# Layer 0's middle taps from a copy moved by GpSimd, and the attention's entrance in another order

## The chip, the cores and the metric

One core of one Trainium2 chip runs the whole program. The metric is the time of one execution on the device in microseconds, lower is better. The kernel before took 947.2 us, the median of three runs (946.99 to 947.26).

## What is computed

The input is x, 16 images of 256 channels and 28 x 28 pixels in fp32. Four layers follow each other:

- Layer 0: a 3x3 convolution of sign(x) with the signs of the weights, scaled by each output channel's mean absolute weight, then a batch norm over all images and pixels, plus x.
- Layer 1: signs, a 3x3 convolution, a 1x1 convolution, PReLUs and two gates made from channel means.
- Layer 2: two convolutions of signs like layer 0's, each with PReLU and a batch norm around it, plus the layer's input, and a last PReLU.
- Layer 3: attention over the 784 pixels of an image with 64 channels for queries, keys and values, and a projection back to 256 channels, plus its input.

```python
def _L3_conv_ref(x, Wq, Wk, Wv, Wp):
    xf = x.reshape(B, C, N)
    q = jnp.einsum('rc,bcn->bnr', Wq, xf)
    k = jnp.einsum('rc,bcn->brn', Wk, xf)
    v = jnp.einsum('rc,bcn->bnr', Wv, xf)
    attn = jax.nn.softmax(jnp.einsum('bnr,brm->bnm', q, k) * scale, axis=-1)
    out = jnp.einsum('bnm,bmr->brn', attn, v)
    return jnp.einsum('cr,brn->bcn', Wp, out).reshape(B, C, H, W) + x
```

A batch norm over all images means that a layer's last moments must be known before the next layer's first image can be made. The stretches between layers are therefore serial.

## The kernel before

**Tiles.** Channels lie on the 128 partitions, in two halves (k = 0, 1). A pixel half is 14 rows, 392 columns (`HN`); an image has two. B = 16, S = 28.

**Convolutions of signs** (`sign_layer`, line 384, used by layer 0 and twice by layer 2). The signs of image i lie as fp16 in `fpads[:, i % 2]`, 30 x 30 with a border of zeros. An image takes 36 matmuls of 392 columns: two channel halves, three rows of taps, three taps c in a row, two pixel halves (line 404). Tap c reads the padded rows from column c on, so the middle tap (c = 1) begins at an odd fp16 column. Two output channels are packed in one sum (`PACK`), which `apart` (line 411) takes apart: ScalarE evicts from PSUM (L420), VectorE makes the other half (L422). `conv_ps` has three PSUM buffers. With `shifted`, images from `direct` on read the middle tap from a second tile that holds the same signs moved by one column, so that it begins at an even one; SyncE makes this copy with a DMA (L434), and the middle taps are then multiplied last within an image (line 398). Layer 2 passes `shifted` in both convolutions, from image 4 and from image 2 on. Layer 0 does not.

**Order.** In `sign_layer` the order on TensorE, ScalarE, VectorE and SyncE is that of the program (`manual_schedule`): for each block the products, the next image's signs, the batch statistics of the block before (`post`), the preparation of later weights (`steps`), and `apart`. GpSimd is not in that set: a scheduler orders its queue. In layer 0, `post0` (line 682) computes batch statistics on VectorE and stores the eviction with a DMA from GpSimd's queue (L688, `n0d`).

**Between layers.** `keep_busy(n)` (line 502, and line 1475 in the attention) multiplies n tiles of zeros on TensorE. Layer 1's tail has several (lines 1108 to 1190), among them `keep_busy(14)` at line 1179 ahead of the matmul of `hidden_a`. `norm` (line 238) makes scale and shift of layer 2's last batch norm: `bn_aggr`, a variance, `rsqrt` (line 144: a Sqrt on ScalarE, a reciprocal and one Newton step on VectorE), then the shifts on ScalarE (L264).

**The attention's entrance** (`attend_unshifted`, from line 1636; here all five engines keep the program's order). Image 0 is finished in two pixel halves: scale, shift, the layer's input x2 and PReLU (lines 1640 to 1649), then queries and keys in one product per half (`queries_keys`, L1486). `keep_busy(8)` follows, then the copies of queries (L1493) and keys (L1497) out of PSUM, `scores(0, 0)` (L1509, with the exponentials at L1513), the values (`project_v`, L1580; four groups of output columns side by side) and their transpose (`turn_v`). Keys lie in chunks of 112 pixels, seven per image. In the loop over images, `scores` of seven chunks, `values` (L1530), sums of exponentials (`sum_up`: chunks 0 to 3 on GpSimd, 4 to 6 on VectorE), denominators and projection are interleaved with the next image's queries, keys and values. `finish_a` (line 1461) scales an image on ScalarE and, from image 2 on, has a DMA from GpSimd's queue add x2 to it (L1466); `finish_b` (line 1468) applies the PReLU on VectorE. The PSUM tag `sc` has two buffers.

Of the kernel before, what the change touches and what calls it, by code (L numbers as in the profile page):

```python
# [27 lines left out]
F32 = mybir.dt.float32  # L28
# [11 lines left out]
P = 128  # L40
B = 16
# [25 lines left out]

STEEP = 1e24


# [20 lines left out]
def forward(ctx: ExitStack, tc: tile.TileContext, d: dict, out: bass.AP, careful: bool):  # L91
# [37 lines left out]

    doubts = const.tile([P, 4 * NB + 10], F32, name="doubts")  # L130
    nc.gpsimd.memset(doubts, 0.0)
# [11 lines left out]

    def rsqrt(name, v, half=None, beside=None):

        r, t = (const.tile(list(v.shape), F32, name=name + q) for q in ("_r", "_t"))
        A.activation(t, v, AF.Sqrt)
        if beside:
            beside()
        V.reciprocal(r, t)  # L150
        tt(t, r, r, ALU.mult)
        if half is not None:
            tt(r, r, half, ALU.mult)
        else:
            V.tensor_scalar(r, r, -0.5, None, ALU.mult)
        tt(t, t, v, ALU.mult)
        V.scalar_tensor_tensor(r, t, -3.0, r, ALU.add, ALU.mult)
        return r
# [78 lines left out]

    def norm(name, moments, gamma, beta, sf=None, then=lambda r: None, late=False):


        half, e = vtile(name + "_half"), vtile(name + "_e")
        V.tensor_scalar(half, gamma, -0.5, None, ALU.mult)
        if sf is not None:

            tt(e, sf, sf, ALU.mult)
            V.tensor_scalar(e, e, 1e-30, 1.0 / EPS, ALU.max, ALU.mult)
            V.reciprocal(e, e)
        m, var = moments()
        v, c, less = vtile(name + "_v"), vtile(name + "_c"), vtile(name + "_less") if late else None
        if sf is not None:  # L250
            tt(v, var, e, ALU.add)
        else:
            V.tensor_scalar(v, var, EPS, None, ALU.add)
        r = rsqrt(name, v, half, (lambda: V.tensor_scalar(less, m, -1.0, None, ALU.mult)) if late else None)
        then(r)
        if not late:
            tt(c, m, r, ALU.mult)
            return r, tt(c, beta, c, ALU.subtract)

        def shift(b):  # L260
            o = vtile(f"{name}_shift{len(made)}")
            made.append(o)
            for k in range(2):
                A.activation(o[:, k:k + 1], r[:, k:k + 1], AF.Identity, bias=b[:, k:k + 1], scale=less[:, k:k + 1])  # L264
            return o

        made = []
        return r, shift
# [114 lines left out]

    def sign_layer(pads, w, temp, room, sign, post, steps, moments, blocks, together=1, shifted=None, direct=2):

# [8 lines left out]
        def products(*js):  # L394
            for j in js:
                pss[j] = conv_ps()
            moved = shifted is not None and blocks[js[0]][0] >= direct
            for taps in ((0, 2), (1,)) if moved else ((0, 1, 2),):
# [29 lines left out]
        def sign_image(i):  # L428

            for r0, r1 in ((0, HR + 1), (HR + 1, S)) if i == 0 else ((0, S),):  # L430
                load = sign(i, slice(r0, r1), lambda k: inner(pads[:, i % 2], k, r0, r1))
                if shifted is not None and i >= direct:
                    to, of = (t[:, i % 2].rearrange("p k a b -> p (k a b)") for t in (shifted, pads))
                    nc.sync.dma_start(out=to[:, 0:-1], in_=of[:, 1:])  # L434
                if load:
                    load()
# [57 lines left out]
    with tc.tile_pool(name="ps_conv", bufs=3, space=PSUM) as psc, \  # L494
# [13 lines left out]
        with tc.tile_pool(name="ph1", bufs=1) as ph:  # L508

            fpads = sign_pads(ph, "vs") if careful else sign_pads(const, None)  # L510
            xs, ns = [None] * B, [None] * B

# [178 lines left out]
            mom = block_moments("l0", PARTS)  # L691
            sign_layer(fpads, w0, temp, room0, sign0, post0, steps, mom, whole_images(PARTS), together=2 if careful else 1)
            for b in range(2):
# [424 lines left out]
            with tc.manual_schedule(engines={ET.PE, ET.DVE, ET.Activation, ET.SP}):  # L1118
# [59 lines left out]
                unit_b(b, 1)  # L1178
                keep_busy(14)
                for k in range(2):  # L1180
# [32 lines left out]
        with tc.tile_pool(name="ph2", bufs=1) as ph:  # L1213
# [36 lines left out]

            def post2(order, alpha, mom, doubt):

# [3 lines left out]
                def post(block, ab):  # L1256
# [33 lines left out]

                    squares = [lambda h=h, m=m: square(h, m) for h, _, m in pieces(block) if not careful]
                    squares_p = [lambda s=s: square_p(*s) for s in by_sums]
                    if i < B - 1:
# [22 lines left out]
            if not careful:  # L1316
# [11 lines left out]
                fpads, w2b, temp, room2, lambda i, rows, out: sign2(pt[i], sg2, bg2, rows, out),  # L1328
                post2(range(B), pv("a2"), mom, doubts[:, 3 * NB:4 * NB]), [], mom, PARTS, shifted=shifted,
            )  # L1330
            late_squares()

            if careful:
                keep_busy(45)
                sg3, bg3 = norm("l2c", mom, pv("g3"), pv("b3"), sf2)
                tt(bg3, bg3, cc, ALU.add)
            else:
                keep_busy(35)
                with tc.manual_schedule(engines={ET.DVE, ET.Activation}):
                    sg3, shift3 = norm("l2c", mom, pv("g3"), pv("b3"), sf2, late=True)  # L1340
                    bg3 = shift3(b3c)
# [78 lines left out]
def attend_unshifted(ctx, tc, d, out, wqk, wv, wp, keys, worst, doubts, flag, pv, finish):  # L1420
# [61 lines left out]

    def queries_keys(b, h, ps):

        for k in range(2):
            T.matmul(  # L1486
                ps[:, h, :HN], lhsT=wqk[:, k, :], rhs=x[b][:, k, h * HN:(h + 1) * HN], start=(k == 0), stop=(k == 1)
            )

    def queries(b, h, ps):  # L1490
# [3 lines left out]

    def keys_to(b, rows, h, ps):
        copy = A.copy if rows else V.tensor_copy
        copy(  # L1497
            keys[b % 2][64 * rows:64 * rows + 64, :, 2 * h:2 * h + 2, 0:GC].rearrange("p c g i -> p g c i"),
            ps[64:P, h, :HN].rearrange("p (g c i) -> p g c i", g=2, i=GC),
        )  # L1500
# [13 lines left out]

    def sum_up(b, *cs):

        for c in cs:
            late, e = c > 3, es[b, c]
            if c in (1, 5):
                sums[b, late] = buf(f"sum{c}", 2)  # L1520
                (V if late else nc.gpsimd).tensor_tensor(sums[b, late], es[b, c - 1], e, ALU.add)
            elif c in (2, 3, 6):
                (V if late else nc.gpsimd).tensor_tensor(sums[b, late], sums[b, late], e, ALU.add)  # L1523

# [49 lines left out]

    def project_v(b):
        ps = one_bank(pssm, "sm")
        for a in range(2):
            for k in range(2):
                for g in range(4):
                    T.matmul(  # L1580
                        ps[32 * g:32 * g + 32, a * GN:(a + 1) * GN], lhsT=wv[:, k, 32 * a:32 * a + 32],
                        rhs=x[b][:, k, g * GN:(g + 1) * GN], start=(k == 0), stop=(k == 1),
                    )
        A.copy(
            vt[:, :, :, 0:GC].rearrange("p c a i -> p a c i"),
            ps[:, 0:2 * GN].rearrange("p (a c i) -> p a c i", a=2, i=GC),
        )
# [48 lines left out]
    with tc.manual_schedule(engines={ET.PE, ET.Activation, ET.DVE, ET.Pool, ET.SP}):  # L1636

        ps = [two_banks(psmi, "mi"), two_banks(pssc, "sc")]
        cuts = [slice(h * HN, h * HN + HN) for h in range(2)]
        for n in cuts:  # L1640
            v = x[0][:, 1, n]
            V.scalar_tensor_tensor(v, v, sg3[:, 1:2], x2[0][:, 1, n], ALU.mult, ALU.add)
        for h, n in enumerate(cuts):
            finish_a(0, n, (0,))
            v, w = (x[0][:, k, n] for k in range(2))
            A.activation(w, w, AF.Identity, bias=bg3[:, 1:2])
            V.tensor_tensor(v, v, x2[0][:, 0, n], ALU.add)
            for k, y in enumerate((v, w)):
                V.scalar_tensor_tensor(y, y, alpha[:, k:k + 1], y, ALU.mult, ALU.max)
            queries_keys(0, h, ps[h])  # L1650
        A.activation(ph.tile([P, 2], F32, name="e"), sg3, AF.Exp, scale=0.0)
        keep_busy(8)
        for h in range(2):
            keys_to(0, 1, h, ps[h])
            queries(0, h, ps[h])
            keys_to(0, 0, h, ps[h])
        finish_a(1)
        scores(0, 0)
        project_v(0)
        finish_b(1, ks=(0,))  # L1660
        turn_v(0)
        finish_b(1, ks=(1,))
        V.transpose(ones.rearrange("p a i -> p (a i)"), turned.rearrange("p a i -> p (a i)"))
        for b in range(B - 1):
            scores(b, 1)
            if b > 0:
                take_values(b - 1)
            if b == 0:
                finish_a(2)
            if b > 1:  # L1670
                project(b - 2, 0)()
            sum_up(b, 1)
            scores(b, 2)
            if b > 0:
                sum_up(b - 1, 6)
            scores(b, 3)
            sum_up(b, 2, 3)
            ps = two_banks(psmi, "mi")
# [17 lines left out]
            if b + 3 < B:  # L1696
                finish_a(b + 3)
            for c in range(4):
                values(b, c)
# [260 lines left out]
```

## Time and profile before

| what | value |
|---|---|
| median of three runs | 947.2 us |
| the profiled execution: time | 948.88 us |
| the profiled execution: span, first to last instruction | 947.1 us |
| mean granted clock of TensorE | 0.996 |
| busy TensorE, VectorE, ScalarE, GpSimd | 98%, 80%, 71%, 15% of the span |
| layer 0's convolution | 10.46 to 109.20 us |
| layer 1 with what precedes it | 109.20 to 464.20 us |
| layer 2's two convolutions | 464.20 to 560.70 and 566.25 to 662.40 us |
| attention with its entrance | 662.40 to 947.1 us |

PE is TensorE, PEld its weight loads, ACT ScalarE, DVE VectorE, POOL GpSimd, SP SyncE. A line of the timeline has start and duration in us, engine, source line, operation, what it writes and reads, its shape, how many were merged, and in brackets the idle time before it with what ended that. In a table by stretches, each engine has its busy time and the number of its instructions.

### The profile page before, as it was taken

To read this page: it belongs to the slowest core of one execution; us is meant where nothing else is said; L and a number is where in the kernel's file an instruction comes from. 1 tells how busy PE (TensorE), PEld (TensorE's weight loads), DVE (VectorE), ACT (ScalarE), POOL (GpSimd) and SP (SyncE) were. 2 spreads that over 40 slices of the span, in tenths; PEclk is the share of its full clock that TensorE was granted. 3 is DMA by queue.
4 is the path that set the end of the run, shared out by engine and by line. 5 is a ranking of instruction groups with operands and counts; after the bars stand their busy time and mean duration, and the time that the engine had idled before them with its cause. 6 is when DMAs were issued, how large, how long until landed. Compare 5 with 4: busy or idle time off the path is not lost.

```text
span 947.1 us, 15041 instructions
## 1 busy us (share of the span) xinstructions
PE 930.2 (98%) x5626; PEld 583.6 (62%) x5632; DVE 759.9 (80%) x1446; ACT 676.1 (71%) x1184; POOL 139.0 (15%) x158
## 2 busy tenths in 40 slices
PE   7999999999999999999999999999999999999996
PEld 3555578888788888887555565556444444444442
DVE  3877888999998889987888887889656868777676
ACT  5766578888888788874777767776766666676653
POOL 2001100000000000000000000000235353443422
PEclk9999999999999999999999999999999999999999
DMA  9877533454543344320566201111142433425212
GB/s 334 292 284 272 187 121 122 173 186 177 198 163 139 139 157 163 143 112 35 207 241 214 113 40 60 79 79 59 31 73 70 97 108 81 125 69 136 69 63 112
DMA packets 39733, 130.70 MB, mean 138 GB/s; under 512 B 4882, under 2 KB 16852, under 8 KB 39652
## 3 DMA queue, kind: packets, MB, share of 16 engines
q1 hardware_dynamic: 33332, 98.31, 28.8%
q0 software_dynamic: 5632, 30.54, 11.8%
q8 instruction: 46, 0.75, 0.3%
q10 hardware_dynamic: 688, 0.80, 0.2%
q14 instruction: 35, 0.29, 0.1%
HBM read 72.67 MB, written 32.11 MB: 111 GB/s over the span
## 4 chain that ended last, share of the span: by engine, by line
PE 95%; DVE 2%; ACT 1%; DMA 1%; issue 0%; SPq 0%; DVEq 0%; ACTq 0%
PE cv L404 31%; PE cv L810 29%; PE sc L1509 8%; PE av L1530 8%; PE cv L937 5%; PE mi L1486 5%; PE sm L1580 2%; PE unused L506 2%; PE mi L1598 2%; PE sm L1530 1%; PE gate L905 1%; DMA st<-in_w_dram 1%; PE hid L713 1%; DVE r L1564 1%; DVE p L1609 0%
## 5 line engine op out<-in xcount | busy, mean ns | idle before, releaser
L810 PE MATMUL cv<-vs,w 128*128 128x392 f32 (+1 forms) x1296 | 272.4, 352 | 0.3 <-DVE vs L141 0.3
L404 PE MATMUL cv<-fpads,wpk 128*128 128x392 f16 (+1 forms) x1458 | 249.3, 327 | 2.2 <-DVE wpk L329 1.2
L404 PEld LDWEIGHTS <-wpk 128*128 128x128 f16 x1782 | 172.1, 97 | 123.6 <-issue 4.3
L810 PEld LDWEIGHTS cv<-vs,w 128*128 128x128 f32 x768 | 143.2, 190 | 6.3
L1513 ACT ACTIVATE es<-sc 128x784 f32<-128x784 f32 x112 | 87.4, 823 | 40.0 <-PE sc L1509 40.0
L810 PEld LDWEIGHTS <-w 128*128 128x128 f16 x768 | 69.4, 99 | 51.9 <-issue 9.1
L1509 PE MATMUL sc<-q,keyswa 64*128 64x392 f32 x448 | 89.9, 513 | 1.2 <-ACT es L1513 0.9
L1530 PE MATMUL av<-es,v 128*64 128x392 f32 x448 | 80.7, 499 | 0.0
L1268 DVE SCALAR_TENSOR_TENSOR p<-ab,vec 128x392 f32<-128x392 int16 (+1 forms) x132 | 78.1, 605 | 0.0
L420 ACT ACTIVATE ab<-cv 128x392 int16<-128x392 f32 (+1 forms) x66 | 32.1, 486 | 56.1 <-PE cv L404 53.2
L1523 POOL TENSOR_TENSOR sum<-sum,es 128x784 f32<-128x784 f32 x32 | 67.2, 2101 | 2.5
L1509 PEld LDWEIGHTS sc<-q,keyswa 64*128 64x128 f32 x448 | 38.9, 186 | 44.0 <-issue 17.1
L404 PE MATMUL cv<-shifted,wpk 128*128 128x392 f16 (+1 forms) x324 | 60.6, 322 | 0.0
L810 PE MATMUL cv<-one_on,w 128*128 128x392 bf16 x240 | 59.4, 329 | 0.0
L965 POOL DMA_DIRECT2D x2d<-x x16 | 8.6, 536 | 345.3 <-DVE x L959 285.0
L1497 DVE COPY keyswa<-mi 64x392 f32<-64x392 f32 x31 | 16.3, 564 | 53.2 <-ACT q L1493 53.2
L1530 PEld LDWEIGHTS av<-es,v 128*64 128x64 f32 x448 | 29.4, 136 | 47.0 <-issue 46.6
L422 DVE SCALAR_TENSOR_TENSOR ab<-ab,cv 128x392 int16<-128x392 int16 (+1 forms) x66 | 36.1, 547 | 27.5 <-ACT ab L420 26.6
L792 ACT CAST vs<-vs 128x840 fp32r<-128x840 bf16 x63 | 54.1, 883 | 2.5 <-DVE vs L141 2.3
L937 PE MATMUL cv<-z,fw 128*128 128x392 f32 x256 | 48.9, 342 | 0.1
L937 PEld LDWEIGHTS cv<-z,fw 128*128 128x128 f32 x256 | 46.1, 188 | 0.9 <-ACT z L929 0.9
L1486 PE MATMUL mi<-p,wqk 128*128 128x392 f32 x124 | 45.1, 506 | 0.1
(325 smaller groups left out, 1532.9 us busy)
## 6 DMA issues: line engine op xcount, KB each, us to landing
xs<-in_x_dram SPq DMA_DIRECT2D x30, 784.0 KB, 5.0
one_on<-vs SPq DMA_DIRECT2D x60, 209.8 KB, 2.9
x2d<-x POOLq DMA_DIRECT2D x16, 784.0 KB, 3.6
out_dram<-p SPq DMA_DIRECT2D x15, 784.0 KB, 3.6
shifted<-fpads SPq DMA_DIRECT2D x26, 449.8 KB, 2.8
p<-x2d POOLq DMA_DIRECT2D x14, 784.0 KB, 6.8
p<-x2d SPq DMA_DIRECT2D x13, 784.0 KB, 5.8
n0d<-n POOLq DMA_DIRECT2D x16, 392.0 KB, 4.4
```

The costliest lines, as they stand in the source:

```text
L404: T.matmul(pss[j][:, n // size if careful else h, :rows * S].rearrange("p (a b) -> p a b", b=S), lhsT=w[:, n, c, :], rhs=src[:, blocks[j][ ...
L420: A.activation(by_halves(ab[:, 1], blocks[j]), ps, AF.Copy, scale=1.0 / PACK)
L422: V.scalar_tensor_tensor(a, b, -PACK, ps, ALU.mult, ALU.add)
L792: copy(v, w)
L810: T.matmul(ps.rearrange("p (a b) -> p a b", b=S), lhsT=w[:, k, c, u, mo * P:(mo + 1) * P], rhs=one_on[:, u, k, :, 0:S] if moved and c == 1 ...
L937: T.matmul(ps[:, h, :HN], lhsT=w[:, k, mo * P:(mo + 1) * P], rhs=z2[b][:, k, h * HN:(h + 1) * HN], start=(k + i == 0), stop=(k + i == 2),)
L1268: V.scalar_tensor_tensor(p, y, alpha[:, mo:mo + 1], y, ALU.mult, ALU.max, accum_out=mom.sums_at(at, mo)[0] if mom.by_sums(at, mo) else None,)
L1486: T.matmul(ps[:, h, :HN], lhsT=wqk[:, k, :], rhs=x[b][:, k, h * HN:(h + 1) * HN], start=(k == 0), stop=(k == 1))
L1509: T.matmul(ps[:, h, :HN], lhsT=chunk[rows], rhs=qs[b][rows], start=True, stop=True)
L1513: A.activation(e, ps[:, :, :HN], AF.Exp, scale=0.125)
L1523: (V if late else nc.gpsimd).tensor_tensor(sums[b, late], sums[b, late], e, ALU.add)
L1530: T.matmul(ps[64 * h:64 * h + 64, :HN], lhsT=w, rhs=e[:, h, :], start=start, stop=stop)
```

## The change

Two separate edits in one. In layer 0, images 2 to 11 get a moved copy of their signs (`moved0`), made by GpSimd with `tensor_copy`; it takes the room of layer 1's tile `vs`. `sign_layer` gets an upper bound `until` and the means of copying as arguments.

At the end of layer 2, `rsqrt` can work by Ln and Exp (`by_log`): exp(-0.5 ln v) replaces Sqrt and reciprocal, the Newton step stays, and two small GpSimd operations note whether the logarithm was in range. The table set with both functions is loaded in layer 2's second convolution, after the squares of image 8's first block; the activation that loaded a table in the entrance is gone. The fillers before it are 31 for 35; in layer 1's tail one is 12 for 14. At the entrance the steps of image 0 are written out by channel half and pixel half, the product of pixel half 1 writes queries and keys to two PSUM tiles, the values are multiplied in two calls of two column groups each, the filler of 8 is gone, keys of half 1 are copied by VectorE in chunks 0 to 1 and 2 to 6, and four scores and two `values` of image 0 are placed ahead of the loop. Chunks 0 and 1 of image 0 are summed on VectorE, not GpSimd. Image 2's `finish_a`, with its DMA, comes after GpSimd's sums of image 0.

```diff
     def rsqrt(name, v, half=None, beside=None, by_log=False):
...
+        if by_log:
+            log = const.tile(list(v.shape), F32, name=name + "_log")
+            A.activation(log, v, AF.Ln)
+            A.activation(r, log, AF.Exp, scale=-0.5)
+            for i, f in enumerate((1.0, -1.0)):
+                n = 4 * NB + 10 + 2 * i
+                nc.gpsimd.tensor_scalar(doubts[:, n:n + 2], log, f / LOG_SPAN, None, ALU.mult)
+        else:
+            A.activation(t, v, AF.Sqrt)
...
-            moved = shifted is not None and blocks[js[0]][0] >= direct
+            moved = shifted is not None and direct <= blocks[js[0]][0] < until
...
-                if shifted is not None and i >= direct:
+                if shifted is not None and direct <= i < until:
                     to, of = (t[:, i % 2].rearrange("p k a b -> p (k a b)") for t in (shifted, pads))
-                    nc.sync.dma_start(out=to[:, 0:-1], in_=of[:, 1:])
+                    copy(out=to[:, 0:-1], in_=of[:, 1:])
...
+            moved0 = None if careful else ph.tile([P, 2, 2, S + 2, S + 2], SIGNS, tag="vs", name="moved0")
...
-            sign_layer(fpads, w0, temp, room0, sign0, post0, steps, mom, whole_images(PARTS), together=2 if careful else 1)
+            sign_layer(fpads, w0, temp, room0, sign0, post0, steps, mom, whole_images(PARTS), together=2 if careful else 1,
+                       shifted=moved0, until=12, copy=nc.gpsimd.tensor_copy)
...
-                keep_busy(14)
+                keep_busy(12)
...
+                    if by_log and i == 8 and r0 == 0:
+                        squares.append(lambda: A.preload_act_table_set("natural_log_exp_and_others"))
...
-                keep_busy(35)
+                keep_busy(31)
...
-                    sg3, shift3 = norm("l2c", mom, pv("g3"), pv("b3"), sf2, late=True)
+                    sg3, shift3 = norm("l2c", mom, pv("g3"), pv("b3"), sf2, late=True, by_log=True)
...
+    def queries_keys_apart(b, h, qps, kps, ks):
+        for k in ks:
+            for i, ps in enumerate((qps, kps)):
+                rows = slice(64 * i, 64 * i + 64)
+                T.matmul(
+                    ps[rows, h, :HN], lhsT=wqk[:, k, rows], rhs=x[b][:, k, h * HN:(h + 1) * HN],
+                    start=(k == ks[0]), stop=(k == ks[1]),
+                )
...
-        for n in cuts:
-            v = x[0][:, 1, n]
-            V.scalar_tensor_tensor(v, v, sg3[:, 1:2], x2[0][:, 1, n], ALU.mult, ALU.add)
-        for h, n in enumerate(cuts):
-            finish_a(0, n, (0,))
-            v, w = (x[0][:, k, n] for k in range(2))
-            A.activation(w, w, AF.Identity, bias=bg3[:, 1:2])
-            V.tensor_tensor(v, v, x2[0][:, 0, n], ALU.add)
-            for k, y in enumerate((v, w)):
-                V.scalar_tensor_tensor(y, y, alpha[:, k:k + 1], y, ALU.mult, ALU.max)
-            queries_keys(0, h, ps[h])
-        A.activation(ph.tile([P, 2], F32, name="e"), sg3, AF.Exp, scale=0.0)
-        keep_busy(8)
-        for h in range(2):
-            keys_to(0, 1, h, ps[h])
-            queries(0, h, ps[h])
-            keys_to(0, 0, h, ps[h])
-        finish_a(1)
+        for k in (1, 0):
+            to_x2(0, k, one)
+        for k in (1, 0):
+            shifted(0, k, one)
+        prelu(0, 1, one)
+        to_x2(0, 1, two)
+        prelu(0, 0, one)
+        finish_a(0, two, (0,))
+        shifted(0, 1, two)
+        add_x2(0, 0, two)
+        for k in (1, 0):
+            prelu(0, k, two)
+        queries_keys(0, 0, ps[0], (1, 0))
+        vps = one_bank(pssm, "sm")
+        project_v(0, vps, range(2))
+        kps = two_banks(pssc, "sc")
+        queries_keys_apart(0, 1, ps[1], kps, (1, 0))
+        project_v(0, vps, range(2, 4))
+        keys_to(0, 1, 0, ps[0])
+        queries(0, 0, ps[0])
+        keys_to(0, 0, 0, ps[0], A.copy)
+        queries(0, 1, ps[1])
+        for cs in (slice(0, 2), slice(2, NC_)):
+            for rows in range(2):
+                keys_to(0, rows, 1, kps, V.tensor_copy, cs)
+        finish_a(1, ks=(0,))
+        to_x2(1, 1)
+        take_v(vps)
+        turn_v(0)
         scores(0, 0)
-        project_v(0)
-        finish_b(1, ks=(0,))
-        turn_v(0)
-        finish_b(1, ks=(1,))
+        scores(0, 1)
+        shifted(1, 1)
+        add_x2(1, 0)
+        for k in range(2):
+            prelu(1, k)
+        sum_up(0, 1, engine=V)
+        scores(0, 2)
+        scores(0, 3)
+        sum_up(0, 2, 3)
+        for c in range(2):
+            values(0, c)
+        finish_a(2)
         V.transpose(ones.rearrange("p a i -> p (a i)"), turned.rearrange("p a i -> p (a i)"))
```

The new helpers: `to_x2` is one pass on VectorE (scale times x plus x2), `shifted` an Identity with the shift as bias on ScalarE, `prelu` and `add_x2` one pass each on VectorE. In the loop, `scores(0, 1)` to `scores(0, 3)`, `sum_up(0, ...)` of chunks 1 to 3 and `values(0, 0)` and `values(0, 1)` are left out, since they have run.

## The prediction

> **What bounds the kernel.** I read the page first: the chain that ended last is TensorE nearly throughout.
>
> ```profile
> PE 95%; DVE 2%; ACT 1%; DMA 1%; issue 0%; SPq 0%; DVEq 0%; ACTq 0%
> ```
>
> So an edit counts only if it makes TensorE's own stream shorter, or takes away filler and waits between two layers. Next came busy time by stretch: layer 0's convolution, layer 2's second one (the same arithmetic), and the attention's entrance.
>
> ```profile
> core 0: us, PE busy (x) PEld busy (x) DVE busy (x) ACT busy (x) POOL busy (x), PEclk, DMA share, GB/s
> 10.46:109.20 98.74, 98.72 (x588) 57.45 (x590) 74.19 (x174) 60.85 (x106) 9.52 (x20) 0.98 0.81 284
> 566.25:662.40 96.15, 96.11 (x595) 57.09 (x594) 80.64 (x167) 68.16 (x152) 0.54 (x3) 1.00 0.17 68
> 670.00:692.10 22.10, 21.57 (x147) 9.92 (x148) 14.12 (x19) 18.04 (x27) 7.47 (x5) 1.00 0.28 48
> ```
>
> The two convolutions have no holes, yet layer 0 takes 2.6 us longer. Part of that is the clock at its start (0.72 in the first 6 us). The rest shows in ScalarE's evictions, which wait for TensorE and so time it; two from layer 0, one image apart, then two from layer 2, one image apart:
>
> ```profile
> 29.65 0.83 ACT L420 ACTIVATE n<-cv 128x784 int16<-128x784 f32 x1 [0.55 <-PE cv L404]
> 35.76 0.82 ACT L420 ACTIVATE n<-cv 128x784 int16<-128x784 f32 x1 [3.07 <-PE cv L404]
> ...
> 626.37 0.50 ACT L420 ACTIVATE ab<-cv 128x392 int16<-128x392 f32 x1 [1.38 <-PE cv L404]
> 632.34 0.50 ACT L420 ACTIVATE ab<-cv 128x392 int16<-128x392 f32 x1 [1.38 <-PE cv L404]
> ```
>
> 6.11 us against 5.97 for the same 36 products. The starts of single matmul records say why: 169.95 ns apart on average in layer 0, in a pattern with one of about 177 in three, and 165.89 where layer 2 reads its middle tap from `shifted`. Layer 2's first two images, which read all taps from `fpads`, also have 169.6 to 169.9. So it is the middle tap's odd column, not layer 0's DMA load.
>
> Then the entrance, TensorE alone:
>
> ```profile
> 662.41 7.50 PE L506 MATMUL unused<-idle 128*128 128x512 bf16 x34
> 670.02 1.55 PE L1486 MATMUL mi<-p,wqk 128*128 128x392 f32 x4
> 671.50 1.58 PE L1486 MATMUL sc<-p,wqk 128*128 128x392 f32 x4
> 672.92 1.67 PE L1479 MATMUL sm<-idle 128*128 128x512 bf16 x7
> 674.84 0.93 PE L1509 MATMUL sc<-q,keyswa 64*128 64x392 f32 x4 [0.24 <-DVE keyswa L1497]
> 675.70 1.53 PE L1580 MATMUL sm<-p,wv 128*32 128x196 f32 x32
> 677.16 1.59 PE L1509 MATMUL sc<-q,keyswa 64*128 64x392 f32 x8
> 679.01 0.93 PE L1509 MATMUL sc<-q,keyswa 64*128 64x392 f32 x4 [0.27 <-ACT es L1513]
> 679.87 2.90 PE L1486 MATMUL mi<-p,wqk 128*128 128x392 f32 x8
> ```
>
> Real work starts at 670.02 and is interrupted by 1.9 us of filler (672.92 to 674.84); after that the stream is dense.
>
> **Layer 0's copies.** Images 2 to 11 get a copy moved by one column; their middle tap reads it last. Gain: 10 images x 36 matmuls x 4.06 ns = 1.46 us, if no copy is late. Each copy (128x1799 fp16) is queued on GpSimd behind one store of n0d (0.54 us), which itself waits for the eviction on VectorE. By the trace, image 6's copy could start at 45.3 (n0d 44.73, signs ready 44.92), and its middle tap is wanted at about 48.1 + 4.0 = 52.1; image 4's 32.5 against 39.9. The cover is 6.8 to 7.4 us per copy.
>
> No row shows such a copy. From below: two GpSimd memsets, 448 and 896 elements, took 0.467 and 0.854, so 0.86 ns an element, 1.6 us. From above: its two-input sums, 784 elements in 1.86 us, 2.37 ns each, 4.3 us. A copy has one input and is nearer to the memset; I take 2.0 to 2.5. Either end is in time. Behind a copy in GpSimd's queue wait the next n0d stores, later by up to one copy; a store's landing frees the `n` buffer for the eviction two images on, and the least time between the two was 3.4 us (39.2 to 42.63), more than a copy.
>
> Here a rule speaks against the change. In the trace a two-input VectorE operation lasts to the end of GpSimd's operation beside it:
>
> ```profile
> 684.05 3.80 POOL L1523 TENSOR_TENSOR sum<-sum,es 128x784 f32<-128x784 f32 x2
> ...
> 686.72 1.96 DVE L1521 TENSOR_TENSOR sum<-es 128x784 f32<-128x784 f32 x1 [0.43 <-ACT es L1513]
> ...
> 702.11 0.93 DVE L1521 TENSOR_TENSOR sum<-es 128x784 f32<-128x784 f32 x1
> ```
>
> The Trainium skill (SBUF — State Buffer, "Who interferes with whom") states it generally: VectorE with two SBUF inputs is shut out while GpSimd reads SBUF, for the whole instruction. By the rule taken for all of VectorE, ten copies cost it up to 25 us, all of its 24.5 us of idle time in layer 0, and the sum would be that of the slower rival below, 951.8. By the rows, what follows each n0d store on VectorE is first 1.97 us of batch statistics (one input); the two-input weight preparation comes about 2.0 us after, the copy starts 0.6 after, so 0.6 to 1.1 us of a 2.0 to 2.5 us copy block anything. VectorE has 74.19 of 98.74 us, 4.6 of 6.1 per image; it stays under. I take no cost and 944.8.
>
> **Layer 1's tail.** The filler `keep_busy(14)` from 456.24 ends at 459.26 (0.216 each) and holds the gate's matmul to 459.36, while its input was there at 458.91. With 12 it starts about 0.33 earlier. VectorE is not released earlier (its products end at 460.94), but the table load behind the gate is; the root then waits for its variance (462.15) and not for the table: 462.19 instead of 462.34. Gain 0.15; bounds 0 and 0.33.
>
> **The root by log and exp.** Sqrt (0.20 on ScalarE) and a reciprocal (0.17) after a hop of 0.03 become Ln and Exp on ScalarE. With durations alike, +0.04; a dependent pair on ScalarE appears in no row, so between +0.0 and +0.2; I take +0.1. The table load of 1.28 us at 670.16 goes away, but it lay in a wait for TensorE (keys copied at 671.67, their product done at 671.57): nothing. It moves into layer 2's second convolution, at image 8, ahead of image 10's signs. Their moved copy landed at 631.97 and was first read at 634.13, so 1.28 fits with 0.87 left. The skill (ScalarE: Activation LUTs, "What ACT_TABLE_LOAD costs") counts 1.28 plus a drain of 1.38; that would stall TensorE 0.5 us. The row of before has the next activation at 671.45, right behind the load, so I take no stall.
>
> **The entrance, step by step** (VectorE passes 0.54 apart, 0.62 long; ScalarE 0.51 apart, 0.61 long, from the 392-column rows). The scale is ready at 667.3; both channel halves of pixel half one are scaled first. Half one is complete near 670.45 (670.31 before) and half two near 672.0 (671.98 before): VectorE and ScalarE gain nothing here. The first product does its ready channel half first and the other from 670.50; its successor can start at 671.33. Then half of the values (the old call had four column groups side by side in 1.46; two groups still need 1.46): 672.79. Queries and keys of half two, side by side in two column halves, as long as the old ones, 1.51: 674.30 (inputs ready at 672.1). Second half of the values: 675.77. Meanwhile ScalarE copies query and keys, and VectorE the first two key chunks (under 0.6 together), so nothing waits but TensorE. Two scores follow, then two that wait for their exponentials (0.70 apart, PSUM has two buffers), to 679.08; two chunks of values, 1.39: the next image's product starts at 680.47. Before, it started at 679.87 with these 1.39 us still to come, 681.26. Gain 0.79: 1.9 of filler and some waits go, 1.46 of extra value time comes.
>
> What is late next: GpSimd. Image 2's accumulate DMA, issued at 681.12 before and landed 6.64 later, now stands behind two sums (3.80) that wait for VectorE's first sum at about 681.2. Issue 685.1, landing 691.8; VectorE, stopped in order at that PReLU, ends it at 692.8, and image 2's product wants it at 694.1. 1.3 us are left; behind it on VectorE stand image 0's sum and image 2's keys, not due before 699. No cost.
>
> **Sum.** 1.46 + 0.15 + 0.79 = 2.40. The profiled execution has a span of 947.1 and a time of 948.88, which would become 946.5; the median is 947.2, hence 944.8.
>
> **Rivals.**
> Entrance lost: the accumulate DMA lands as late as the slowest in the trace (7.42) and the sums are stretched to their longest (2.48 each): 692.9 + about 0.9, image 2's product waits 0.7 to 0.8. Remaining 1.6: 945.6. Against: 1.3 of slack.
> Copies late: the middle tap waits in every image and layer 0 gains nothing, only 0.94 is left: 946.2. Against: 7 us of cover.
> Slower: the lock. If a copy takes 2.9 us or more, VectorE's 4.6 plus (copy less 1.4) passes 6.1 and it falls behind; from 3.9 the lag of 1 us per image eats the 10 us that PSUM's three buffers give (image 4 evicted at 44.4, image 7 starting at 54.2). At 4.3, 13 us of lag: TensorE stalls 3 and, after four images of recovery, layer 0's moments come 4 later: +7 - 2.4, 951.8. For it: no row of a copy. Against: one input.
> Better: TensorE's remaining waits at the entrance (0.35 before the first product's second part, 0.2 to 0.3 at the scores) vanish and the root is free: 944.0.
>
> **Numbers.** Forecast 0.60, better 0.08, entrance lost 0.14, copies late 0.09, lock 0.09. A measurement can tell about 0.2% (1.9 us), so faster is below 945.3: most of the forecast, the better case and a little of the lost entrance, 0.64; slower is the lock, 0.09; the same 0.27. The range 943.6 to 946.6 takes in all but the lock and some tails.
>
> **What would show it.** In layer 0, evictions 5.97 apart from image 2 to 11 and 6.11 else; GpSimd copies of 2.0 to 2.5 us; VectorE's weight preparation stretched a little. The table load inside layer 2's second convolution without a hole on TensorE. First product of the attention near 669.3 less 1.6, and 0.8 less between layer 2's last product and image 1's second scores. I am wrong if copies exceed 3 us, if evictions keep 6.11, or if TensorE waits for image 2's PReLU.

## The result and the profile after

The changed kernel takes 944.99 us (median of 15 runs, 944.40 to 945.59); the kernel before, beside it, 947.20. The ratio is 0.9974, with a 95% interval of 0.9967 to 0.9982: 2.2 us less, where 2.4 were predicted. The profiled execution of the changed kernel has a time of 945.37 and a span of 943.6.

The chain that ended last, from the page of the changed kernel:

```profile
PE 90%; DVE 6%; ACT 1%; DMA 1%; SPq 1%; issue 0%; DVEq 0%; ACTq 0%
```

VectorE's share rose from 2% to 6%, but it did not get slower. Before, the first product of the attention followed directly on filler, so the chain ran back through TensorE. Now the filler ends 0.38 us before that product, which waits for VectorE. The chain therefore goes back through VectorE's PReLUs and batch statistics to the eviction at 632.66. From there to 667.6, apart from 1.7 us of ScalarE at the root and the shift, the chain is VectorE's: by the profile it sets the end of layer 2, not TensorE. No run tried that.

The same three stretches by busy time, now 10.46 to 106.63, 563.59 to 659.58 and 22.1 us of the entrance (columns as before: PE, PEld, DVE, ACT, POOL, then the granted clock):

```profile
10.46:106.63 96.17, 95.88 (x588) 56.59 (x590) 79.59 (x174) 60.62 (x106) 26.58 (x30) 1.00 0.82 293
563.59:659.58 95.99, 95.95 (x595) 57.09 (x594) 80.34 (x167) 69.47 (x153) 0.54 (x3) 1.00 0.17 68
666.60:688.70 22.10, 21.72 (x146) 9.57 (x146) 11.99 (x20) 17.13 (x26) 5.47 (x4) 1.00 0.22 39
```

Layer 0's stretch is 2.57 shorter, and nearly as short as layer 2's. GpSimd's busy time there went from 9.52 to 26.58 (ten copies), VectorE's from 74.19 to 79.59, with the same 174 instructions: work on VectorE is held longer. Two of ScalarE's evictions in layer 0, one image apart:

```profile
70.18 0.82 ACT L430 ACTIVATE n<-cv 128x784 int16<-128x784 f32 x1 [0.65 <-PE cv L414]
76.16 0.82 ACT L430 ACTIVATE n<-cv 128x784 int16<-128x784 f32 x1 [2.94 <-PE cv L414]
```

5.98 instead of 6.11. This sign of the prediction holds only for the later evictions: up to image 8 they are 2.9 to 9.1 apart, while the products of images 2 to 11 end 5.98 apart throughout. ScalarE works in order and stands behind other waits there, and the cover shrinks. Before the eviction of image 4 it waits 3.48 us for a DMA with weight rows (1.52 before the change), and the signs of image 6 (second line) are complete at 45.70, 0.35 ahead of that image's first product at 46.05. In the kernel before, 2.9 were left:

```profile
41.59 0.84 ACT L357 ACTIVATE sts<-sts 128x768 f32<-128x768 f32 x1 [3.48 <-DMA sts<-in_w_rows_dram]
44.10 1.59 ACT L537 ACTIVATE fpads<-xs 128x784 f16<-128x784 f32 x2
```

Not all of the 2.57 is gained: the profiled execution of before had a window of 3.4 us at half the clock at the start of layer 0, which that of after lacks (mean clock there 0.98 against 1.00). By the ends of the ten images' products, which lie behind the window, the copies bring 61.18 - 59.84 = 1.34.

The entrance on TensorE:

```profile
666.61 1.91 PE L1501 MATMUL mi<-p,wqk 128*128 128x392 f32 x4 [0.38 <-DVE p L1684]
668.45 1.52 PE L1608 MATMUL sm<-p,wv 128*32 128x196 f32 x16
669.90 1.54 PE L1511 MATMUL sc<-p,wqk 128*64 128x392 f32 x8
671.37 1.52 PE L1608 MATMUL sm<-p,wv 128*32 128x196 f32 x16
672.82 1.59 PE L1535 MATMUL sc<-q,keyswa 64*128 64x392 f32 x8
674.69 1.64 PE L1535 MATMUL sc<-q,keyswa 64*128 64x392 f32 x8 [0.29 <-ACT es L1539]
677.74 2.90 PE L1501 MATMUL mi<-p,wqk 128*128 128x392 f32 x8
```

No filler is left inside, and the values stand there twice, 1.5 us each time: two column groups take as long as four did.

### The profile page after: what moved, and what is told of

It reads as the page before. It is cut to its first block, busy times and chain, and to the rows that moved or that the text cites. A ratio compares the mean times of both kernels' runs of the same rounds, so it can differ in the third digit from the quotient of the medians.

```text
span 943.6 us, 15045 instructions
## 1 busy us (share of the span) xinstructions
PE 926.7 (98%) x5617; PEld 581.9 (62%) x5622; DVE 766.3 (81%) x1448; ACT 676.0 (72%) x1184; POOL 155.4 (16%) x169
## 4 chain that ended last, share of the span: by engine, by line
PE 90%; DVE 6%; ACT 1%; DMA 1%; SPq 1%; issue 0%; DVEq 0%; ACTq 0%
PE cv L822 29%; PE cv L414 27%; PE sc L1535 8%; PE av L1556 8%; PE cv L949 5%; PE mi L1501 5%; PE sm L1608 3%; PE mi L1630 2%; DVE p L1280 1%; DVE l2c_fin L1288 1%; PE sm L1556 1%; DMA xs<-in_x_dram 1%; PE unused L516 1%; PE gate L917 1%; PE hid L725 1%; DVE r L1590 1%
## 5 line engine op out<-in xcount | busy, mean ns | idle before, releaser
L414 PE MATMUL cv<-fpads,wpk 128*128 128x392 f16 (+1 forms) x1338 | 228.6, 325 | 2.0 <-DVE wpk L339 1.2
```

Source lines behind the costliest of these rows:

```text
L414: T.matmul(pss[j][:, n // size if careful else h, :rows * S].rearrange("p (a b) -> p a b", b=S), lhsT=w[:, n, c, :], rhs=src[:, blocks[j][ ...
```

## Experiments

Times are medians; "before" is 947.2 in each comparison. Gains read from traces are stretches between the same two products of two executions.

| kernel | us | ratio to before, 95% |
|---|---|---|
| e1_copies_alone | 946.04 | 0.9988 (0.9981 to 0.9994) |
| e2_no_copies | 946.32 | 0.9992 (0.9985 to 0.9998) |
| e3_unread | 946.27 | 0.9990 (0.9981 to 0.9998) |
| e4_two_inputs | 956.31 | 1.0094 (1.0079 to 1.0109) |
| e5_until16 | 944.66 | 0.9969 (0.9958 to 0.9980) |
| e6_dma | 946.67 | 0.9990 (0.9982 to 0.9999) |
| e7_tail_sqrt | 945.08 | 0.9977 (0.9971 to 0.9984) |
| e8_values_whole | 944.22 | 0.9968 (0.9956 to 0.9980) |
| e9_two_inputs_unread | 955.47 | 1.0093 (1.0078 to 1.0108) |
| e10_dma_first | 944.97 | 0.9977 (0.9969 to 0.9986) |
| e11_best | 944.13 | 0.9970 (0.9959 to 0.9981) |
| e12_best_direct | 943.60 | 0.9964 (0.9950 to 0.9977) |

My theory: TensorE's own stream got shorter in two separate places, and nothing is given back. The rivals to it: the gain of layer 0 is only the clock of one execution; the lock between GpSimd and VectorE takes part of it; TensorE now and then waits for image 2.

### The two halves of the change

**e1_copies_alone**: the kernel before with the `sign_layer` hunks and this call:

```diff
-sign_layer(fpads, w0, temp, room0, sign0, post0, steps, mom, whole_images(PARTS), together=2 if careful else 1)
+sign_layer(..., together=2 if careful else 1, shifted=moved0, until=12, copy=nc.gpsimd.tensor_copy)
```

> The kernel before with layer 0's ten GpSimd copies and nothing else of the change. Theory: each of the ten images saves 36 x 4.06 ns, 1.46 us by the single records and 1.34 by the changed kernel's trace, and nothing comes back later: 1.3 to 1.5 us below the kernel before, 945.8. In the trace the ten images are 5.98 apart, layers 1 and 2 and the entrance are as before (L2's last product to image 2's queries and keys 32.8). Rival (the gain of layer 0 is only the lower clock at the start of the profiled execution of before, and the whole 2.2 us come from the later parts): no difference from the kernel before, 947.2.

Measured: 946.04, 1.13 below before. The products of its moved images end 5.99 apart, layer 2's last product to image 2's queries and keys 32.79, as before (32.77). The clock rival (all of layer 0's gain was a window of low clock) falls: the interval excludes no gain.

**e2_no_copies**: the changed kernel with that call as it was.

> The changed kernel without layer 0's copies, all else kept. Theory: the entrance gives 0.63 to 0.79, layer 1's tail 0.14, a hole of 0.16 in layer 2 was chance: 0.8 to 0.95 below the kernel before, 946.3, and 1.3 above the changed kernel. Rival (copies gain nothing): as the changed kernel, 945.0.

Measured: 946.32, 0.85 below before and 1.33 above the changed kernel. The two parts (1.13 and 0.85) add up to 1.98 of the 2.21; what is missing lies within their intervals, so no disturbance of one by the other is seen. This run's profiled execution also shows what I had priced as the lost entrance. GpSimd, VectorE and TensorE around image 2's PReLU (L1486, two channel halves; L1545 is a sum on GpSimd, L1499 the last six matmuls of the product of queries and keys):

```profile
683.66 0.94 POOL L1479 DMA_DIRECT2D p<-x2d  x1
691.11 3.58 DVE L1486 SCALAR_TENSOR_TENSOR p<-p,vec 128x784 f32<-128x784 f32 x2 [4.20 <-DMA p<-x2d]
691.96 1.89 POOL L1545 TENSOR_TENSOR sum<-es 128x784 f32<-128x784 f32 x1 [3.01 <-ACT es L1537]
694.75 2.24 PE L1499 MATMUL mi<-p,wqk 128*128 128x392 f32 x6 [1.03 <-DVE p L1486]
```

The DMA landed at 691.09, 7.43 after its start (6.60 to 7.01 in the other executions with this order). GpSimd's sum then began at 691.96, 0.1 before the second half of the PReLU, which lasted 2.63 instead of 1.03, and TensorE, which needs that half from the product's third matmul on, waited 1.03. In all nine executions with this order the sum begins 12.87 after image 1's product. In the other eight the PReLU's second half began first, and the sum was the one held: 2.0 to 2.4 instead of 1.84. So it is a race, and the later one of the two waits.

### What the copies cost

**e3_unread**: the copies are made, but TensorE reads the middle tap from the odd column.

```diff
-            moved = shifted is not None and direct <= blocks[js[0]][0] < until
+            moved = read and shifted is not None and direct <= blocks[js[0]][0] < until
...
-                       shifted=moved0, until=12, copy=nc.gpsimd.tensor_copy)
+                       shifted=moved0, until=12, copy=nc.gpsimd.tensor_copy, read=False)
```

> The changed kernel in which GpSimd still makes the ten copies but TensorE goes on reading the middle tap from the odd column, so that only the price of the copies is left. Theory (the copies lie beside VectorE's slack; stretched operations there cost nothing): as the run without copies, 946.3, within 0.2. Rival (the lock on VectorE takes part of the gain, by late evictions): up to 0.5 above that run; the images of layer 0 would be further apart than 6.12.

Measured: 946.27, the time without copies; layer 0's last product at 107.75 against 107.77. Within the intervals the ten copies cost nothing, though VectorE is held, and the 1.28 to the changed kernel come with reading them. (The order of the taps changes with that too. That the odd column makes the difference is read from the prediction's single records, one in three of which takes about 177 ns; no run parts it from order and tile.)

VectorE's groups between 17 and 100 us of the span (busy us, mean ns | idle), first before, then the changed kernel:

```profile
L329 DVE SCALAR_TENSOR_TENSOR wpk<-sg 128x384 f16<-128x384 bf16 x5 | 2.7, 540 | 0.0
L422 DVE SCALAR_TENSOR_TENSOR n<-n,cv 128x784 int16<-128x784 int16 x14 | 13.6, 970 | 20.5 <-ACT n L420 20.5
```

```profile
L339 DVE SCALAR_TENSOR_TENSOR wpk<-sg 128x384 f16<-128x384 bf16 x5 | 4.6, 928 | 0.0
L432 DVE SCALAR_TENSOR_TENSOR n<-n,cv 128x784 int16<-128x784 int16 x14 | 13.6, 968 | 12.6 <-ACT n L430 12.4
```

A weight step beside a copy takes 0.93 instead of 0.54. VectorE's wait for evictions is the cover: 20.5 us of it before, 12.6 after.

**e4_two_inputs**: a longer occupation of GpSimd with the same result, by a sum with a zero that is read for every element.

```diff
-                       shifted=moved0, until=12, copy=nc.gpsimd.tensor_copy)
+                       shifted=moved0, until=12, copy=lambda out, in_: nc.gpsimd.tensor_tensor(
+                           out, in_, nil[:, 0:1].to_broadcast([P, 1799]), ALU.add))
```

> The changed kernel with each moved copy made by a two-input sum on GpSimd (signs plus a zero read again for every element), which should take about 4.3 us by 2.37 ns an element where the copy takes 1.70. The tiles hold the same. By the slower rival's price (lock from 2.9 us on, stalls from 3.9): VectorE falls behind by about 1.4 us per image, TensorE stalls in layer 0's later images, about 3 us, and layer 0's moments come about 4 later: near 952. By the theory that only the two-input weight preparation is held, and that VectorE catches up in the images that have none: 945.0 to 946. The trace shows which VectorE operations end with GpSimd's.

Measured: 956.31, 11.3 above the changed kernel. The sum took 3.20, not 4.3. By the rival's own arithmetic 3.20 would not yet stall TensorE; it did, more than the rival had for 4.3. **e9_two_inputs_unread** leaves these sums in but reads the odd column, to part lateness of the copy from the lock.

> The changed kernel with the 3.20 us two-input copies, which are made but not read: the middle tap is read from the odd column. It parts the 11.3 us that the two-input copies cost into the price of a late copy and the price of the lock on VectorE. Theory A (TensorE's waits stood in front of moved taps, so the copy's lateness is most of it): near the kernel whose plain copies are not read, 946.3, and at most 950. Theory B (the lock makes evictions and moments late by itself): 952 or more, and the stretch from layer 0's last product to layer 1's first again near 10 us, not 6.24.

Measured: 955.47 (953.30 to 957.35). Theory A falls. e3 reads the odd column too and has the plain copies, so e9 minus e3 is the price of the lock: 9.2 us. That leaves at most about 2 of the 11.3 for late copies. In the trace, layer 0's last product is at 112.75 (107.75 in e3) and layer 1's first 8.94 behind it (6.24 in the changed kernel). At two stops of TensorE the profiled execution also has a window of 3.41 us in which the granted clock is one half; an estimate from length and clock is up to 1.7 us each, on top of the stops. How TensorE comes to stop once, in e9:

```profile
49.71 3.20 POOL L706 TENSOR_TENSOR moved<-fpads,nil 128x1799 f16<-128x1799 f16 x1
50.75 2.58 DVE L339 SCALAR_TENSOR_TENSOR wpk<-sg 128x384 f16<-128x384 bf16 x1
55.09 3.20 POOL L706 TENSOR_TENSOR moved<-fpads,nil 128x1799 f16<-128x1799 f16 x1
56.13 2.58 DVE L594 TENSOR_SCALAR st<-st 128x768 f32<-128x768 f32 x1
58.74 0.42 ACT L605 ACTIVATE w<-st 128x256 f16<-128x256 f32 x1 [6.51 <-DVE st L594]
60.62 0.80 ACT L430 ACTIVATE n<-cv 128x784 int16<-128x784 f32 x1
61.33 1.60 ACT L539 ACTIVATE fpads<-xs 128x784 f16<-128x784 f32 x2
62.23 1.01 PE L414 MATMUL cv<-fpads,wpk 128*128 128x392 f16 x5 [2.53 <-ACT fpads L539]
```

Two of VectorE's steps, 0.54 and 0.55 long by themselves, each last to 0.4 behind the end of a sum on GpSimd (52.91 and 58.29). ScalarE stands in order behind the second and is idle 6.51 us, of which the two holds are 4.1; in e3 the wait at the same place is 2.49. Only then come the eviction, the next image's signs and TensorE's product. And between 17 and 100 us of e9:

```profile
L699 DVE BATCH_NORM_STATS2 l_parts<-n 128x6 f32<-128x392 int16 x44 | 21.7, 556 | 0.4
L339 DVE SCALAR_TENSOR_TENSOR wpk<-sg 128x384 f16<-128x384 bf16 x4 | 10.3, 2571 | 0.0
```

Batch statistics are not held at all (556 ns, as before); a weight step is held until the sum has ended. The prediction had this rule of the Trainium skill (SBUF — State Buffer, "Who interferes with whom") for two inputs only. The page also says that one-input forms such as `tensor_scalar` can use both port pairs and then contend with GpSimd, and L594 is a `tensor_scalar`: the rows agree with the page.

**e6_dma**: the copies by SyncE's DMA, as in layer 2.

```diff
-                       shifted=moved0, until=12, copy=nc.gpsimd.tensor_copy)
+                       shifted=moved0, until=12)
```

> The changed kernel in which SyncE moves layer 0's copies by DMA, as in layer 2, not GpSimd. It asks whether GpSimd was needed: the DMA engines are at a share of 0.81 in layer 0, so a copy of 450 KB may land late (4 to 8 us where layer 2's takes 2.8) and SyncE's queue waits for the signs ahead of the loads of x. If it lands within the 6.8 us of cover: 945.0, as changed, and VectorE's operations keep their plain lengths. If not: TensorE waits in each image, from 1 to 3 us each, 955 to 970. Half way I expect the second, in some images only: 948.

Measured: 946.67 (944.78 to 949.01, an unusually wide spread), 1.7 above the changed kernel. VectorE's weight steps are back at 541 ns, but the DMA share between 17 and 100 us rises from 0.84 to 0.96, a copy needs 6.5 us from issue to landing in the median, and two middle taps waited for one (0.35 and 0.15). These waits are 0.5 of the 1.7; for the rest the profile shows no late copy. GpSimd was the better place by the medians, and the late copies point to the memory queues as the place with less room than VectorE.

**e5_until16**: `until=16` for `until=12`.

> The changed kernel with moved copies for images 2 to 15 instead of 2 to 11. Theory: four more images at 0.134 (measured) to 0.146 (single records) each: 0.5 to 0.6 below the changed kernel, 944.4; evictions 5.98 apart also in images 12 and 13. Rival (a copy in GpSimd's queue ahead of the last stores and of the last image's moments makes layer 0's end late): the stretch from layer 0's last product to layer 1's first grows beyond 6.24 and the time is 945.0 or above.

Measured: 944.66, 0.33 below the changed kernel. In the trace layer 0's last product comes 0.86 earlier and layer 1's first 0.66. About 0.3 of that is the execution and not the edit: in e8 and e10, whose layer 0 is the changed kernel's, the last product comes 0.3 to 0.4 earlier as well. Of the 0.5 to 0.6 that four images bring, 0.20 is given back at once, half of it before the moments are known and half in the steps of layer 1's first image.

### The entrance and the small parts

**e7_tail_sqrt**: filler 14 in layer 1's tail, `late=True` without `by_log`, no table load in layer 2, and ahead of the first keys' copy:

```diff
+        A.activation(ph.tile([P, 2], F32, name="e"), sg3, AF.Exp, scale=0.0)
         keys_to(0, 1, 0, ps[0])
```

> The changed kernel with its two small parts undone: filler of 14 in layer 1's tail, and the root by Sqrt and reciprocal, with Exp's table loaded at the entrance behind half two's shift. Theory: the tail's stretch to layer 2's first product 18.31 again (+0.14), the root's chain 0.03 to 0.04 shorter, the table load hidden in ScalarE's wait for the first product or up to 0.3 late for the keys' copy: 0.1 to 0.4 above the changed kernel, 945.1 to 945.4. Rival (the table load is on the path, as ScalarE copies keys and queries right behind it): 1.3 us more in the entrance, 946.4.

Measured: 945.08, within the spread of the changed kernel, and the rival's 946.4 falls. The trace shows the parts: layer 1's last product to layer 2's first 18.31 again (18.17 changed), layer 2's last product to the first of the attention 7.28 (7.32 changed), and image 1's queries and keys 11.13 behind that in both. The table load of 1.28 us is hidden in either place.

**e8_values_whole**: the values of image 0 in one call.

```diff
         vps = one_bank(pssm, "sm")
-        project_v(0, vps, range(2))
         kps = two_banks(pssc, "sc")
         queries_keys_apart(0, 1, ps[1], kps, (1, 0))
-        project_v(0, vps, range(2, 4))
+        project_v(0, vps)
```

> The changed kernel with image 0's values in one call of four column groups behind the product of half two, not two calls of two groups around it. It tests the sum's term of 1.46 us for the second call. Theory: half two is ready at 669.1 in the changed kernel's profiled execution, 0.65 behind the first product's end, so TensorE waits 0.65 and saves 1.52: first scores 0.65 to 0.85 earlier than now, image 1's queries and keys too, 0.65 below the changed kernel, 944.3. Rival (the half in between is cover that was needed, the keys' copies come too late for the first scores): no gain, 945.0.

Measured: 944.22, 0.77 below the changed kernel. TensorE of this kernel:

```profile
666.36 1.91 PE L1501 MATMUL mi<-p,wqk 128*128 128x392 f32 x4 [0.38 <-DVE p L1684]
668.36 1.54 PE L1511 MATMUL sc<-p,wqk 128*64 128x392 f32 x8
669.82 1.53 PE L1608 MATMUL sm<-p,wv 128*32 128x196 f32 x32
671.29 1.59 PE L1535 MATMUL sc<-q,keyswa 64*128 64x392 f32 x8
```

From the first product to the first scores 4.93 us, 6.21 in the changed kernel: 1.28 less, more than the 0.65 to 0.85 I expected, because the wait for half two never came. Its product begins 0.09 after the first has run out (668.27), since it multiplies channel half 1 first, which is ready at 668.30; channel half 0 follows on VectorE while TensorE is on half 1. The half of the values put in between covered nothing. The median shows 0.77 of the 1.28, which the intervals allow.

**e10_dma_first**: image 2's `finish_a` ahead of GpSimd's sums.

```diff
+        finish_a(2)
         sum_up(0, 2, 3)
         for c in range(2):
             values(0, c)
-        finish_a(2)
```

> The changed kernel with image 2's accumulate DMA ahead of GpSimd's two sums of image 0, not behind them. Two executions show TensorE's gap at image 2's product: none where the DMA landed 6.63 after issue, 1.03 where it took 7.43 and the sum that started at its landing held VectorE's PReLU to 2.63. Theory (the lost-entrance rival holds in part of the executions): DMA issued about 2 us earlier, no such gap in any, median 0.1 to 0.5 below the changed kernel. Rival (it is rare): equal to the changed kernel within 0.1.

Measured: 944.97, no difference. The DMA started 2.0 us after image 1's product, not 4.6, and the second half of PReLU 2 ended 3.6 before the product's third matmul, which wants it, not 1.25. The gap of e2 is real but was rare: one of the nine profiled executions in which the DMA stood behind the sums.

### The versions the runs point to

**e11_best** joins e5, e8 and e10. **e12_best_direct** also begins the moved copies earlier:

```diff
-                       shifted=moved0, until=16, copy=nc.gpsimd.tensor_copy)
+                       shifted=moved0, until=16, direct=1, copy=nc.gpsimd.tensor_copy)
...
-                       shifted=shifted, direct=4)
+                       shifted=shifted, direct=2)
...
-                [], mom, PARTS, shifted=shifted,
+                [], mom, PARTS, shifted=shifted, direct=1,
```

> The changed kernel with three edits that the runs point to: copies up to image 15, the values in one call, image 2's accumulate DMA ahead of the two sums. By the traces 0.54 + 1.28 + 0 (in executions without the gap): 943.2; by the medians of the single runs 0.33 + 0.77 + 0.02: 943.9.

> The version before with moved copies from image 1 on in layer 0 and in layer 2's second convolution, and from image 2 on in layer 2's first: four more images at 0.146, 0.58 below it, 942.6 to 943.3. Rival (a copy of the first images lands after its middle tap is wanted): a wait of TensorE in that image, up to 2 us, and no gain.

Measured: 944.13 and 943.60. e11 misses its expectation by a little: its span is 2.1 below the changed kernel's, but the stretch from layer 0's last product to layer 1's first grew by 0.47 (6.71). Its trace names the new wait, on VectorE's first step of layer 1:

```profile
109.39 1.03 DVE L772 SCALAR_TENSOR_TENSOR xs<-n,l_r,xs 128x784 f32<-128x784 int16 x1 [0.42 <-DMA n<-n0d]
```

Image 0's reload from `n0d`, which was there in time when layer 0 ended later, is what is late next; TensorE waited 0.41 behind its filler. In e12 the reload came in time (6.33). e12 (943.14 to 943.67) is the fastest kernel run here, its slowest run below the changed kernel's fastest, but it misses its 942.6 to 943.3 too, and its 0.53 to e11 lies within e11's spread (943.28 to 945.40). Layer 0 became shorter (98.48 against 98.66). Layer 2's second convolution did too (95.72 against 96.04), but e11 has an extra 0.19 between two products there, so the image brings 0.13. Layer 2's first one did not (96.31 against 96.27). There TensorE was 0.26 ahead of e11 at the twelfth image, whose copy landed no earlier: 68.4 us behind the convolution's first product in both. The middle tap waited for it:

```profile
529.41 0.82 PE L414 MATMUL cv<-shifted,wpk 128*128 128x392 f16 x4 [0.23 <-DMA shifted<-fpads]
```

TensorE then waited 0.4 for the signs of the next image, and the two images' gain was gone.

## Why the prediction was right, and where it was off

| step | predicted | measured |
|---|---|---|
| layer 0's copies | -1.46 | -1.34 (trace), -1.13 (e1), -1.33 (e2 against changed) |
| one copy on GpSimd | 2.0 to 2.5 us | 1.70 (1.83 once) |
| price of the lock | 0 | 0 (e3 equals e2) |
| layer 1's tail | -0.15 | -0.14 (e7 +0.14) |
| root by log and exp | +0.1 | +0.04 |
| table load in layer 2 | no stall | no stall |
| entrance, with the root | -0.79 | -0.63 to image 2's product (e2 -0.85 with the tail) |
| slack at image 2's PReLU | 1.3 us | 1.25, and missing once |
| sum | -2.40 | -2.21 |

**The copies** were right in mechanism. The term was 0.12 too large: an image took 5.984 us, not the 5.97 of layer 2, and 6.12 before. The copies took 1.70 and not 2.0 to 2.5, read from a memset's and a sum's time per element.

**The lock** was rightly left at nothing, and the reading of the rows behind it held: a copy runs mostly beside batch statistics, which are not held, and a weight step behind them loses 0.39. What failed is the rival's price, "from 3.9 the lag of 1 us per image eats the 10 us that PSUM's three buffers give". I summed VectorE's load per image and gave TensorE the buffers as reserve. At 3.20 that sum is barely over the pace (4.6 + 1.8 against 6.1), yet 9.2 us were lost. ScalarE waits in order for VectorE's weight steps ahead of its own evictions and signs, so two held steps reach TensorE within two images. The deciding point lies between 1.70 and 3.20, not at 3.9; the copy, shorter than I took it, stayed below that, which was luck in part: at the 2.5 us that I also allowed, this is open.

**The entrance** gained what was said within 0.16, but its largest term, "1.46 of extra value time", was taken as the price of not waiting for half two. e8 shows no such wait, so 1.28 of it was avoidable. I had half two "near 672.0" on the clock of before as one moment, when its channel half 1 came 0.5 us sooner and the product begins with that.

**The slack** at image 2 was nearly right (1.25 for 1.3), though for a simpler picture than the runs show. The landing came as predicted (688.93, predicted 689.0 on this execution's clock). I counted one PReLU of about 1 us behind it; there are two of 1.03, of which the product needs the second only from its third matmul on, 0.76 after its start. What I left out is the race with GpSimd's sum. In e2 the DMA took 7.43, 0.8 more than in the changed kernel's execution, which would have left 0.45; the second half, held 1.6, came too late. The rival's price of 0.7 to 0.8 was 1.03 where it happened, so in that one execution the prediction's last sign of being wrong appeared.

The remaining 0.16 us of the trace's difference is one place in layer 2's second convolution of before's profiled execution where two products start 0.31 apart instead of 0.15; that of after lacks it. Five of the fourteen profiled executions have such a place, with and without the change, so it is no gain.

## What to carry to other kernels

A cheap copy on an idle engine is worth its place when what it locks has slack, but count that slack along the in-order queues (who waits for the held instruction, and what stands behind it there), not as an engine's sum of busy time. Before putting work into a gap, look whether the gap is there: a product that starts with the operand half that is ready first may leave none. And work that gets ahead, within a layer or at its end, can uncover a transfer that was just in time for what comes next.

## What the runs showed of the hardware

- An image of 36 matmuls of 392 fp16 columns lasts 6.12 us where 12 of them begin at an odd column of the moving operand, and 5.98 where all begin at an even one. The copy may come from GpSimd or from a DMA (e6), if it is in time.
- GpSimd copies 128x1799 fp16 in 1.70 us (0.94 ns an element) and adds a zero, read again for every element, in 3.20 (1.78 ns), less than the 2.37 ns of its fp32 sums.
- Beside GpSimd's sums, VectorE's two-input operations and a one-input fp32 `TENSOR_SCALAR` lasted until these had ended (2.57 and 2.58 instead of 0.54 and 0.55), and where VectorE began first, GpSimd's sum was the one held (2.0 to 2.4 instead of 1.84); batch statistics (556 ns) and the operation with one input in PSUM (962 against 970) did not change.
- Ln and Exp, the second on the first's result, start 0.23 us apart on ScalarE, 0.20 long each: the hop between them is 0.03.
- Besides the last microseconds of every execution, TensorE's granted clock fell to one half for single windows of 3.4 to 6.8 us. In e4 and e9 TensorE stood still three times for 2.5 to 4.0 us, and each time such a window begins between 1 us before and 1.2 us after the end of the stop. After the stop at the start of layer 0 (0.8 to 1.7 us) one begins in three of the fourteen executions (before, e4, e7). e7, with the same layer 0 as e8 and e10, takes 1.6 us longer there than these two, which have no window. Whether standing still is the cause was not tried.
